# An adaLN transformer block on one core: all row tiles of the attention product in pairs, each pair by half-size products

## The chip, the cores and the metric

The kernel runs on one core of a Trainium2 chip. Its time is the device time of one execution in microseconds (us). Before the change it is 756.9 us (median of three runs, 756.22 to 757.13). The engines are TensorE (PE, with its weight loads shown apart as PEld), VectorE (DVE), ScalarE (ACT), GpSimd (POOL) and SyncE (SP, which here only issues transfers).

## The reference

For each of 8 batches, with x of 1024 rows by 256 columns, all in float32:

```python
mod = (_silu(c) @ wmod).reshape(8, 6, 1, 256)
sa, ca, ga, sb, cb, gb = (mod[:, n] for n in range(6))
ga, gb = (sign(g) * maximum(abs(g), 0.25) for g in (ga, gb))
h = layernorm(x) * (1 + ca) + sa
x = x + ga * (softmax((h * w_lhs) @ (h * w_rhs).T) @ h)
h = layernorm(x) * (1 + cb) + sb
x = x + gb * (relu(h @ W1 + b1) @ W2 + b2)
```

W1 is 256 by 1024, W2 is 1024 by 256. So one batch has a score matrix of 1024 by 1024, its softmax, the product of that with a 1024 by 256 matrix, and the two layers of the FFN.

## The kernel before, in words

**Stages.** A batch is cut into eight row tiles of 128 rows, i = 0 to 7 (`for b`, `for i` at the end of the kernel). In stage (b, i) the kernel computes the scores of the tile two ahead (`direct`, line 412), mirrors them into the part of the symmetric score matrix that was not computed (`mirror`, lines 435 and the transfer behind it), takes the row maximum (`row_max`, 463), turns it (`max_turn`, 468), subtracts (`subtract`, 475) and exponentiates (`exponent`, 484) the tile one ahead, and multiplies a tile's weights with the values (`xg`). The values carry a 257th column of ones, which gives the softmax's denominator. Beside this, in the same eight stages, runs the FFN of the batch before, one half of 512 rows (g = 0 or 1) in four stages: i = 0, 1 (and 4, 5) hold its first layer, two groups c each, and i = 2, 3 (and 6, 7) its second layer. Its result is turned back to rows and added to x some stages later (`y_gate`, `y_turn`, `y_add`, `y_out`). The next batch's normalisation and its turned copies (`prepare_norm` 281, `prepare_turn_apart` 342, `prepare_blocks` 322, `x_plus` and `xg_times` 642) are spread over the stages too.

**Products of weights and values.** A row tile can go alone: `product` (501) is 8 matmuls of 128 x 257, and `product_out` (513, 515) scales and adds on VectorE. Or two row tiles i and i+1 go together as a 2 x 2 block product by seven half-size products (a Strassen-Winograd scheme). `pair_begin` (549) computes two of the seven and ScalarE copies one (555); `pair_begin_sum` (561) adds them; `left_sums` forms four sums of the two weight tiles in place on GpSimd (565 and 575 to 577, 128 x 512 each); `pair_end` (593) computes the other five products with the sums of the values in `tsum` (`right_sums`, 534); `pair_out` (608 to 621) combines on VectorE; `pair_stats` takes the layer norm's statistics of both tiles. In the batches after the first, tiles 0 and 5 go alone, and (1, 2), (3, 4), (6, 7) are pairs. Batch 0 uses single products only.

**The FFN's first layer** goes by the same scheme, four groups c per half. `pair_products` computes six of seven products into `pa`, `pb`, `pc`; ScalarE copies `pa` into `kept` (747); `pair_sums` adds on VectorE (762, 765, 768, 771); `pair_last` writes the seventh product over the first half of `pa`, VectorE adds it (779), and GpSimd adds the fifth product, `kept[:, hi]`, to two halves of the result f with one instruction of 128 x 512 (780). `pair_relu` (789, 790) follows on ScalarE, and `pair_turn` (799 to 802) forms the second layer's sums on GpSimd. The second layer is `y_first` and `y_second` (806).

**What sets the order.** Each engine runs its instructions in the order of the program; `pin` adds that order as a dependency, so nothing is reordered. A buffer of the pool `ps_a` (four PSUM banks, shared by `pa`, `pb`, `pc`, `po`, `pp`, `pq`, `pr`, `ya` and the like) is given to the next tile when the last reader of the one four allocations earlier is done. `s1`, `W` and `f` have a single buffer each, `kept` and `u` two. Transfers of `move` are issued by SP in order: four writes to DRAM and one read back; with `hurry=False` the read is put off until after the next such transfer. GpSimd's adds of rows (`later`) wait in a queue from which `spare()` takes one at a time.

Of the kernel before, what the change touches and what calls it, by code (L numbers as in the profile page):

```python
# [11 lines left out]
F32 = mybir.dt.float32  # L12
AF = mybir.ActivationFunctionType
ALU = mybir.AluOpType
# [3 lines left out]
P = 128  # L18
# [6 lines left out]
def adaln_block_kernel(  # L25
# [435 lines left out]
    def row_max(b, i):  # L461
        m = work.tile([P, 1], F32, tag="m", name=f"m_{b}_{i}")
        nc.vector.tensor_reduce(m, score_row(b, i), AX.XY, ALU.max)  # L463
        max_t[b, i] = m
# [95 lines left out]
        rows = slice(P, P + XS)  # L560
        nc.vector.tensor_tensor(W[:, 0, rows], pp[:, XS : 2 * XS], W[:, 1, rows], ALU.add)

    def left_sum(b, i):
        s1 = two_t["s1"] = work.tile([P, TH, P], F32, tag="s1", name=f"s1_{b}_{i}", bufs=1)
        nc.gpsimd.tensor_tensor(s1, *halves(pT_t[b, i + 1]), ALU.add)

    def left_sums(b, i):


        if "s1" not in two_t:  # L570
            left_sum(b, i)
        (a11, a12), (a21, a22) = halves(pT_t[b, i]), halves(pT_t[b, i + 1])
        s1 = two_t["s1"]
# [154 lines left out]
    def pair_products(b, g, c, between=None):  # L728

        if c == 0:  # L730
            ffn["f"] = two.tile([P, NI, HALF], F32, tag="f", name=f"f_{b}_{g}", bufs=1)
            if b < B - 1:
                ffn["ft"] = two.tile([P, 3, NH, H2], F32, tag="ft", name=f"ft_{b}_{g}", bufs=1)
        hT, hs = ffn["hT", g]
        n = ts(c, P)
        s1, a22 = (w1[:, k, ds((c + NH) * P, P)] for k in range(2))

        pool, tag = (ps_s, "s") if b == B - 1 else (ps_a, "a")
        pa = ps_a.tile([P, HALF], F32, tag="a", name=f"pa_{b}_{g}_{c}")
# [7 lines left out]
        nc.scalar.copy(kept, pa)  # L747
        mm(pb[:, lo], w1s[:, 0, n], hs[:, 1])
        mm(pb[:, hi], w1s[:, 1, n], hs[:, 2])
        mm(pc[:, lo], w1[:, 1, n], hT[:, 1, lo])  # L750
        mm(pc[:, hi], a22, hT[:, 0, hi])
        if between:
            between()
        pairs[c] = pa, pb, pc, kept

    def pair_sums(b, g, c):
        pa, pb, pc, kept = pairs[c]
        f = ffn["f"]
        u = work.tile([P, H2], F32, tag="u", name=f"u_{b}_{g}_{c}", bufs=2)
        pairs[c] = pa, kept, u  # L760
        far = f[:, c + NH, hi]
        nc.vector.scalar_tensor_tensor(
            u, pb[:, lo], b1_col(c), kept[:, lo], ALU.add, ALU.add
        )
        nc.vector.scalar_tensor_tensor(  # L765
            far, pb[:, hi], b1_step[:, c : c + 1], u, ALU.add, ALU.add
        )
        nc.vector.scalar_tensor_tensor(
            f[:, c, lo], pc[:, lo], b1_col(c), kept[:, lo], ALU.add, ALU.add
        )  # L770
        nc.vector.tensor_tensor(f[:, c + NH, lo], pc[:, hi], far, ALU.add)

    def pair_last(b, g, c):


        pa, kept, u = pairs.pop(c)
        f = ffn["f"]
        mm(pa[:, lo], w1s[:, 2, ts(c, P)], ffn["hT", g][0][:, 1, hi])
        nc.vector.tensor_tensor(f[:, c, hi], pa[:, lo], u, ALU.add)  # L779
        nc.gpsimd.tensor_tensor(  # L780
            f[:, c::NH, hi],
            f[:, c::NH, hi],
            kept[:, None, hi].to_broadcast([P, 2, H2]),
            ALU.add,
        )

    def pair_relu(c):
# [362 lines left out]
    for b in range(B):  # L1150
        for i in range(NT):
# [63 lines left out]
            if first:  # L1215

                ub, ug = (b - 1, 0) if i >= TH else (b - 2, 1)
                back = i % TH == 0 and ub >= 0
                pair_products(fb, fg, c, turn_max)
                if i == 0:  # L1220
                    ffn_rstd(b - 1, 1)
                if i == 4:
                    y_gate(fb)
                    if b + 1 < B:
                        prepare_rstd(b + 1, 1)
                if i == TH + 1:
# [1 line left out]
                pair_sums(fb, fg, c)  # L1228
                if (b, i) == (1, 0):
                    subtract(*late)  # L1230
                if i == 4:
                    y_turn(fb, 0)
                if ahead:
                    mirror(*ahead)
                pair_last(fb, fg, c)
                if i == 0 and back:
                    for q in range(2):
                        y_add(ub, ug, q)
                if i == TH + 1:
                    pair_turn(c - 1)  # L1240
                if late and i != 4 and (b, i) != (1, 0):
                    subtract(*late)
                pair_products(fb, fg, c + 1, (lambda: max_turn(*extra)) if extra else None)
# [9 lines left out]
                        prepare_turn_apart(b + 1, 1, 0)  # L1253
                if i == 1:
                    exponent(*late)
                    left_sum(b, i)
                elif i == 4 and b + 1 < B:
                    prepare_norm(b + 1, 1)
                    x_plus(b + 1, 1)
# [15 lines left out]
                    weights(*late)  # L1275
                if ahead and ahead != extra:
                    row_max(*ahead)
                pair_turn(c)
                if i == 0:
                    pair_relu(c + 1)  # L1280
                    pair_turn(c + 1)
                if i == 4:
                    for q in range(2):
                        y_add(ub, ug, q)
                if c > 0:
                    pair_relu(c + 1)
                    pair_turn(c + 1)
            else:
                half = i % TH - 2
                if i == NT - 2:  # L1290
                    for q in (1, 3):
                        if (b, q) in two_t:
                            pair_stats(b, q)
                if i == 2:
                    left_sums(b, 1)
                elif i == 3:
                    pair_begin(b, i, turn_max)
                elif i == 6:
                    pair_begin(b, i, lambda: (max_turn(*late), weights(*late)))
                elif not ahead:  # L1300

                    pair_end(b, i - 1)
                    pair_out(b, i - 1)
                    pair_stats(b, i - 1)
                if half:
                    y_second(fb, fg, turn_max if i == NT - 1 else None)
                else:
                    y_first(fb, fg, turn_max if i == 2 else None)
                if ahead:
# [4 lines left out]
                    ffn_rstd(b, 0)  # L1314
                elif i == NT - 1 and b == B - 1:
                    ffn_rstd(b, 1)
                if i in (3, 6):
                    pair_begin_sum(b, i)
                if i == 2:
                    weights(*late)  # L1320
                elif i == 6:
                    left_sums(b, i)
                spare()
                early(b, i)
# [6 lines left out]
                if ahead:  # L1331
                    row_max(*ahead)
                if half:
                    y_second_sums(fb)
                    if i == NT - 1:
                        y_gate(fb)
                    elif b + 1 < B:
                        prepare_stats(b + 1, 1)
                else:
                    y_first_sums()  # L1340
                spare()
            if extra:
                subtract(*extra)
            if i == NT - 1 and 0 < b < B - 1:
                y_turn(fb, fg, True)
            turns(b, i)
            norms(b, i)
            if extra:
# [103 lines left out]
```

## Time and profile before

| | |
|---|---|
| median of three runs | 756.9 us (756.22 to 757.13) |
| the profiled execution | 756.93 us, span 755.1 us |
| TensorE busy | 749.1 us |
| VectorE busy | 574.9 us |
| GpSimd busy | 570.9 us |
| ScalarE busy | 374.9 us |
| one batch in the middle (253.26 to 343.70) | 90.44 us |

The page lists for each engine its busy time; the chain that ended last follows the work back from the end of the program, at each step to what released it; the groups of instructions give for each line the engine, the tiles (output <- inputs), the count, the busy time, the mean duration of one in ns and the idle time before it; the timeline lists single instructions with start and duration in us. A busy time counts an instruction's whole duration, and successive ones overlap a little, so that where the cost of one instruction more is wanted, the time from start to start is the better measure.

### The profile page before, as it was taken

The page shows a single profiled execution, that of the slowest core. Times are in us where ns is not written, and L with a number is a line of the kernel's source. Part 1 is how long each engine was busy: PE and PEld are TensorE (multiplying, and loading weights), DVE is VectorE, ACT ScalarE, POOL GpSimd, SP SyncE. Part 2 cuts the span into 40 slices and gives each one's busy share as a digit, 9 for nine tenths or more (in the row PEclk, how much of TensorE's full clock was granted, in tenths as well). Part 3 has the DMA queues.
Part 4 walks back from the last instruction along what each step waited for, and adds up shares of the span by engine and source line. Part 5 has one row for each costly group of instructions (what it writes and reads, how often), then busy time and mean ns, then how long its engine had stood idle before and what let it go on. Part 6 is the DMA issues. An engine that isn't in the chain of part 4 may idle for free.

```text
span 755.1 us, 11883 instructions
## 1 busy us (share of the span) xinstructions
PE 749.1 (99%) x3876; PEld 623.4 (83%) x3876; DVE 574.9 (76%) x1259; ACT 374.9 (50%) x688; POOL 570.9 (76%) x658
## 2 busy tenths in 40 slices
PE   8999999999999999999999999999999999999998
PEld 4686889788897888888888878988889788888887
DVE  7787879778796879968878688876889777685632
ACT  4554646635375454745546444563546535252521
POOL 3762796878968798788877699777996888669741
PEclk9999999999999999999999999999999999999999
DMA  9033442455443453445534555245553354133220
GB/s 308 16 112 98 131 133 74 135 178 152 127 120 123 153 153 110 147 118 158 164 99 119 153 154 161 74 127 172 155 152 85 119 166 133 50 91 126 84 85 28
DMA packets 106213, 95.21 MB, mean 126 GB/s; under 512 B 29700, under 2 KB 98848, under 8 KB 106152
## 3 DMA queue, kind: packets, MB, share of 16 engines
q1 hardware_dynamic: 98408, 85.81, 38.6%
q10 hardware_dynamic: 7744, 8.65, 3.7%
q8 instruction: 30, 0.49, 0.3%
q14 instruction: 31, 0.25, 0.1%
HBM read 50.62 MB, written 43.81 MB: 125 GB/s over the span
## 4 chain that ended last, share of the span: by engine, by line
PE 96%; DMA 1%; DVE 1%; ACT 1%; issue 0%
PE psc L412 16%; PE pa L726 11%; PE po L501 10%; PE pr L593 7%; PE pb L726 7%; PE pc L726 7%; PE yc L806 6%; PE ya L806 6%; PE yb L806 6%; PE pq L593 5%; PE pp L549 5%; PE py L916 4%; PE yd L806 3%; DMA wm<-in_L_wmod_dram 1%; PE pm L468 1%; PE pmr L194 0%
## 5 line engine op out<-in xcount | busy, mean ns | idle before, releaser
L412 PE MATMUL psc<-rT,lT 128*128 128x512 f32 (+3 forms) x384 | 134.8, 487 | 0.0
L780 POOL TENSOR_TENSOR f<-f,kept 128x512 f32<-128x512 f32 x64 | 81.5, 1274 | 42.8 <-DVE f L779 20.1
L419 ACT COPY sc<-psc 128x512 f32<-128x512 f32 (+3 forms) x96 | 44.7, 476 | 119.9 <-PE psc L412 113.0
L484 ACT ACTIVATE pT<-pT 128x1024 f32<-128x1024 f32 x64 | 67.6, 1056 | 70.6 <-DVE pT L475 70.5
L475 DVE TENSOR_TENSOR pT<-sc,pm 128x1024 f32<-128x1024 f32 x64 | 77.3, 1208 | 29.3 <-PE pm L468 13.7
L412 PEld LDWEIGHTS psc<-rT,lT 128*128 128x128 f32 x384 | 66.4, 191 | 37.2 <-issue 25.6
L501 PE MATMUL po<-xg,pT 128*128 128x257 f32 x352 | 80.6, 380 | 0.0
L463 DVE TENSOR_REDUCE m<-sc 128x1 f32<-128x1024 f32 x64 | 77.4, 1209 | 2.2 <-ACT sc L419 1.8
L501 PEld LDWEIGHTS po<-xg,pT 128*128 128x128 f32 x352 | 66.2, 190 | 10.0 <-issue 0.7
L747 ACT COPY kept<-pa 128x512 f32<-128x512 f32 x64 | 37.4, 584 | 69.3 <-PE pa L726 69.1
L726 PE MATMUL pb<-hs,w1s 128*128 128x256 f32 x256 | 65.9, 380 | 0.1
L726 PE MATMUL pc<-hT,w 128*128 128x256 f32 x256 | 65.7, 379 | 0.0
L880 POOL TENSOR_TENSOR x<-x,Y 128x512 f32<-128x512 f32 x28 | 35.1, 1276 | 29.3 <-DMA Y<-D_y 29.3
L789 ACT ACTIVATE f<-f 128x512 f32<-128x512 f32 x64 | 39.8, 622 | 34.7 <-POOL f L780 34.7
L642 POOL TENSOR_TENSOR x<-x,rows 128x256 f32<-128x256 f32 x64 | 44.8, 732 | 13.8 <-ACT rows L1022 10.6
L726 PEld LDWEIGHTS pb<-hs,w1s 128*128 128x128 f32 x256 | 48.5, 190 | 7.3 <-DVE f L765 0.8
L726 PEld LDWEIGHTS pc<-hT,w 128*128 128x128 f32 x256 | 48.6, 190 | 6.7
L806 PE MATMUL yc<-f,w2s 128*128 128x256 f32 x224 | 51.3, 379 | 0.0
L435 DVE STREAM_TRANSPOSE Tm<-sc 128x896 f32<-128x896 f32 (+6 forms) x49 | 34.3, 701 | 20.3 <-ACT sc L419 19.6
L806 PEld LDWEIGHTS yc<-f,w2s 128*128 128x128 f32 x224 | 41.5, 190 | 8.1 <-issue 2.9
L549 PEld LDWEIGHTS pp<-xg,pT 128*128 128x128 f32 x336 | 41.9, 192 | 5.1 <-DVE st_b L241 1.4
L799 POOL TENSOR_TENSOR ft<-f 128x256 f32<-128x256 f32 x56 | 40.8, 729 | 6.8 <-ACT f L790 6.8
(166 smaller groups left out, 1821.1 us busy)
## 6 DMA issues: line engine op xcount, KB each, us to landing
D_f<-T_f SPq DMA_DIRECT2D x60, 128.0 KB, 2.5
X_f<-D_f SPq DMA_DIRECT2D x15, 512.0 KB, 3.7
D_a<-T_a SPq DMA_DIRECT2D x56, 128.0 KB, 2.8
D_y<-T_y SPq DMA_DIRECT2D x56, 128.0 KB, 2.9
Y<-D_y SPq DMA_DIRECT2D x14, 512.0 KB, 3.4
out_dram<-x SPq DMA_DIRECT2D x14, 512.0 KB, 4.4
X_a<-D_a SPq DMA_DIRECT2D x13, 512.0 KB, 3.4
x<-in_L_attn_x_dram ACTq DMA_DIRECT2D x12, 512.0 KB, 3.4
```

The lines of the kernel that those rows point to most:

```text
L412: nc.tensor.matmul(psc[:, : hi - lo], lhsT=lT_t[b, i // TH][:, k, ts(i % TH, P)], rhs=rT_t[b, n][:, k, lo - n * HALF : HALF], start=(k == ...
L419: nc.scalar.copy(score_row(b, i)[:, lo // V : hi // V, :], psc[:, : hi - lo].rearrange("p (n v) -> p n v", v=V),)
L463: nc.vector.tensor_reduce(m, score_row(b, i), AX.XY, ALU.max)
L475: nc.vector.tensor_tensor(pT.rearrange("p j (a v) -> p j a v", v=V), score_columns(b, i), pm[:, :P].rearrange("p (j a v) -> p j a v", j=1, ...
L484: nc.scalar.activation(pT_t[b, i], pT_t[b, i], AF.Exp)
L501: nc.tensor.matmul(po[:, : D + 1], lhsT=pT[:, t, :], rhs=xg_t[b][:, t, 0 : D + 1], start=(t == 0), stop=(t == NT - 1),)
L549: nc.tensor.matmul(out, lhsT=lhs[:, t, :], rhs=xg_t[b][:, h * TH + t, P : P + XS], start=(t == 0), stop=(t == TH - 1),)
L593: nc.tensor.matmul(out, lhsT=lhs[:, t, :], rhs=rhs[:, t, :], start=(t == 0), stop=(t == TH - 1),)
L642: queue.append(lambda: nc.gpsimd.tensor_tensor(out, in0, row, op))
L726: nc.tensor.matmul(out, lhsT=lhsT, rhs=rhs, start=True, stop=True)
L780: nc.gpsimd.tensor_tensor(f[:, c::NH, hi], f[:, c::NH, hi], kept[:, None, hi].to_broadcast([P, 2, H2]), ALU.add,)
L806: nc.tensor.matmul(out, lhsT=lhs(c), rhs=rhs(c), start=(c == 0), stop=(c == NH - 1))
```

## The change

All eight row tiles of the batches after the first go in pairs: (0, 1), (2, 3), (4, 5), (6, 7). `left_sum` and `left_sums` become one function, called in i = 1, 2, 5, 6 for the pairs beginning at 0, 2, 4, 6. The first two products of a pair are computed in i = 0, 2, 4, 6 and the other five in i = 1, 3, 5, 7. To make room, the gate and the turn of the FFN's second half move from the end of i = 7 into i = 0 of the next batch, its addition to x (`y_add`) from i = 0 to i = 1 (and that of the first half from i = 4 to i = 5), the output one stage later, `right_sums` a little earlier in i = 7, and the statistics of each pair to stages where they are placed by hand. In the FFN, VectorE adds `kept[:, hi]` to `u` with one more instruction per group (new line 767), so that the seventh product's sum holds it; GpSimd's instruction then covers one half of f (128 x 256) and not two. Batch 0 keeps its single products.

```diff
-    def left_sum(b, i):
+    def left_sums(b, i):
         s1 = two_t["s1"] = work.tile([P, TH, P], F32, tag="s1", name=f"s1_{b}_{i}", bufs=1)
         nc.gpsimd.tensor_tensor(s1, *halves(pT_t[b, i + 1]), ALU.add)
-
-    def left_sums(b, i):
-        if "s1" not in two_t:
-            left_sum(b, i)
         (a11, a12), (a21, a22) = halves(pT_t[b, i]), halves(pT_t[b, i + 1])
...
         nc.vector.tensor_tensor(f[:, c + NH, lo], pc[:, hi], far, ALU.add)
+        nc.vector.tensor_tensor(u, kept[:, hi], u, ALU.add)
...
         nc.gpsimd.tensor_tensor(
-            f[:, c::NH, hi],
-            f[:, c::NH, hi],
-            kept[:, None, hi].to_broadcast([P, 2, H2]),
-            ALU.add,
+            f[:, c + NH, hi], f[:, c + NH, hi], kept[:, hi], ALU.add
         )
...
+                returned = i % TH == 1 and ub >= 0
                 pair_products(fb, fg, c, turn_max)
                 if i == 0:
                     ffn_rstd(b - 1, 1)
+                if back:
+                    y_gate(ub)
                 if i == 4:
-                    y_gate(fb)
...
                 pair_sums(fb, fg, c)
...
-                if i == 4:
-                    y_turn(fb, 0)
+                if back:
+                    y_turn(ub, ug)
                 if ahead:
                     mirror(*ahead)
+                if i % TH == 1:
+                    left_sums(b, i - 1)
                 pair_last(fb, fg, c)
-                if i == 0 and back:
-                    for q in range(2):
-                        y_add(ub, ug, q)
-                if i == TH + 1:
+                if i % TH == 1:
                     pair_turn(c - 1)
+                if (b, i) == (B - 1, 5):
+                    pair_stats(b, 2)
...
-                    left_sum(b, i)
...
+                if returned:
+                    for q in range(2):
+                        y_add(ub, ug, q)
                 pair_turn(c)
                 if i == 0:
                     pair_relu(c + 1)
-                    pair_turn(c + 1)
-                if i == 4:
-                    for q in range(2):
-                        y_add(ub, ug, q)
...
-                if i == NT - 2:
-                    for q in (1, 3):
-                        if (b, q) in two_t:
-                            pair_stats(b, q)
+                if i == NT - 2 and b < B - 1:
+                    pair_stats(b, 2)
                 if i == 2:
-                    left_sums(b, 1)
+                    pair_begin(b, i)
                 elif i == 3:
-                    pair_begin(b, i, turn_max)
+                    turn_max()
                 elif i == 6:
                     pair_begin(b, i, lambda: (max_turn(*late), weights(*late)))
-                elif not ahead:
-
+                else:
+                    turn_max()
                     pair_end(b, i - 1)
-                    pair_out(b, i - 1)
-                    pair_stats(b, i - 1)
+                    if not ahead:
+
+                        pair_out(b, i - 1)
+                        pair_stats(b, i - 1)
...
-                if i in (3, 6):
+                if not half:
                     pair_begin_sum(b, i)
-                if i == 2:
-                    weights(*late)
-                elif i == 6:
+                    if i == 2:
+                        weights(*late)
                     left_sums(b, i)
...
                 if half:
+                    if i == NT - 1 and ahead:
+                        pair_out(b, i - 1)
                     y_second_sums(fb)
-                    if i == NT - 1:
+                    if i == NT - 1 and b == B - 1:
                         y_gate(fb)
-                    elif b + 1 < B:
-                        prepare_stats(b + 1, 1)
+                    elif i == 3:
+                        pair_stats(b, 0)
+                        if b + 1 < B:
+                            prepare_stats(b + 1, 1)
                 else:
                     y_first_sums()
+                    if i == NT - 2:
+                        pair_stats(b, 4)
...
             if i == NT - 1 and 0 < b < B - 1:
-                y_turn(fb, fg, True)
+                while queue:
+                    spare()
+                right_sums(b + 1, range(4))
...
-            if i in (0, 5):
-                product(b, i)
-                product_out(b, i)
-            elif i == 1:
+            if i in (0, 4):
                 pair_begin(b, i)
                 pair_begin_sum(b, i)
-            elif i == 3:
-                left_sums(b, i)
-            elif i in (2, 4) or i == NT - 1 and ahead:
+            elif i in (1, 3, 5):
                 pair_end(b, i - 1)
                 pair_out(b, i - 1)
-                if i == NT - 1:
-                    assert not queue
-                    right_sums(b + 1, range(4))
-                if i == NT - 1 or b == B - 1:
-                    pair_stats(b, i - 1)
+            elif i == NT - 1 and ahead:
+                pair_stats(b, i - 1)
             late = ahead if ahead != extra else None
-            if first and back:
+            if first and returned:
                 y_out(ub, ug)
```

More of the change, by code (lines that the diff above doesn't have):

```diff
@@ L561, in pair_begin_sum @@
         nc.vector.tensor_tensor(W[:, 0, rows], pp[:, XS : 2 * XS], W[:, 1, rows], ALU.add)
-    def left_sum(b, i):
+    def left_sums(b, i):
         s1 = two_t["s1"] = work.tile([P, TH, P], F32, tag="s1", name=f"s1_{b}_{i}", bufs=1)
         nc.gpsimd.tensor_tensor(s1, *halves(pT_t[b, i + 1]), ALU.add)
-    def left_sums(b, i):
-        if "s1" not in two_t:
-            left_sum(b, i)
         (a11, a12), (a21, a22) = halves(pT_t[b, i]), halves(pT_t[b, i + 1])
-        s1 = two_t["s1"]
         add = nc.gpsimd.tensor_tensor
@@ L1289, in adaln_block_kernel @@
                 half = i % TH - 2
-                if i == NT - 2:
-                    for q in (1, 3):
-                        if (b, q) in two_t:
-                            pair_stats(b, q)
+                if i == NT - 2 and b < B - 1:
+                    pair_stats(b, 2)
                 if i == 2:
-                    left_sums(b, 1)
+                    pair_begin(b, i)
                 elif i == 3:
-                    pair_begin(b, i, turn_max)
+                    turn_max()
                 elif i == 6:
                     pair_begin(b, i, lambda: (max_turn(*late), weights(*late)))
-                elif not ahead:
+                else:
+                    turn_max()
                     pair_end(b, i - 1)
-                    pair_out(b, i - 1)
-                    pair_stats(b, i - 1)
+                    if not ahead:
+                        pair_out(b, i - 1)
+                        pair_stats(b, i - 1)
                 if half:
-                    y_second(fb, fg, turn_max if i == NT - 1 else None)
+                    y_second(fb, fg)
                 else:
```

## The prediction

> **What bounds the kernel now.** I read the page first, then the time by stages, then the rows around the edits.
>
> ```profile
> span 755.1 us, 11883 instructions
> PE   749.1 (99%) x3876; PEld 623.4 (83%) x3876; DVE 574.9 (76%) x1259; ACT 374.9 (50%) x688; POOL 570.9 (76%) x658
> PE 96%; DMA 1%; DVE 1%; ACT 1%; issue 0%
> ```
>
> TensorE (PE) is busy 99% and is 96% of the chain that ended last. So work taken off TensorE is time won, as long as nobody makes it wait, and every wait made for it is time lost. The other engines look loose, but only as averages. By stages (one batch from 343.70; i=0, 1, 4, 5 are the stages with the FFN's first layer):
>
> ```profile
> 343.70:355.90 12.20, 12.20 (x55) 9.95 (x54) 10.70 (x25) 5.85 (x12) 12.04 (x12) 1.00 0.52 151
> 355.90:366.01 10.11, 10.11 (x55) 8.37 (x53) 8.32 (x19) 5.80 (x11) 8.28 (x11) 1.00 0.68 201
> 366.01:379.21 13.20, 13.20 (x80) 11.36 (x78) 9.45 (x21) 6.30 (x13) 12.73 (x17) 1.00 0.46 128
> 387.58:399.06 11.48, 11.48 (x74) 10.60 (x73) 10.79 (x27) 8.43 (x16) 7.60 (x8) 1.00 0.22 55
> 399.06:409.13 10.07, 10.07 (x51) 8.87 (x50) 9.11 (x21) 5.93 (x11) 6.87 (x8) 1.00 0.71 214
> ```
>
> Columns: length, then busy time of PE, PEld, DVE, ACT, POOL, then clock. In i=0 and i=2 GpSimd (POOL) is full to 0.2 and 0.5 us, and in i=4 VectorE (DVE) to 0.7: little room for work that moves there. The period is 90.43 us, TensorE packed throughout.
>
> **The gain.** A whole product is 16 `po` records, 3.46 us from the first to the next group (352.44 to 355.90). A pair is 16 `pp` records, 1.78 us (364.22 to 366.01), and 40 `pq`/`pr` records, 4.46 us (374.75 to 379.21): 6.24 against 6.92 for two products. Products 0 and 5 go in batches 1 to 7, one more pair comes: 7 x 0.69 = 4.8 us. Batch 0 is unchanged. Without a wait, 756.9 - 4.8 = 752.1. The profiled execution took 756.93 us (span 755.1, 1.8 around it), the median 756.9, so both serve as one base.
>
> **GpSimd and VectorE, in sum.** GpSimd's add to f falls from 128x512 (1.27) to 128x256 (0.73), 8 per batch: -4.3. The fourth set of left sums adds four ops of 1.27 (1.33 with the turn-round): +5.3. Net +1 on some 74 of 90. VectorE gets eight adds L767 (u = kept + u, 128x256): nearest rows L771 and L779, 128x256, next start after 0.31 to 0.33, so 2.6; a pair_out (2.6, 399.55 to 402.17) and a W sum (0.2) for two product_outs (0.7 each): about +4 on 73. Neither is a bound as a sum; place decides. L767 has both inputs in SBUF, L771 not. VectorE rows with such inputs stretch while GpSimd works: L655 (128x4) took 143/408/1084 ns (min/median/max), and at 352.19 lasted 0.38, until just after GpSimd began another op at 352.51. So an L767 costs 0.31 to 0.31+1.27 (one GpSimd 128x512 op); I take 0.33, plus a lock where GpSimd's left sums run beside it.
>
> The Trainium skill ("SBUF — State Buffer", Who interferes with whom) says that a VectorE op with two SBUF inputs and a GpSimd op that reads SBUF exclude each other for a whole instruction. By that, with GpSimd 82% busy, each L767 would wait about half an op, an estimate of 0.5 us; by the row above mostly less.
>
> **Stages 4 and 5, the largest loss.** In i=5 TensorE's last product of c=2 (`pa`, w1s) overwrites a buffer that ScalarE (ACT) must first copy (`kept`). ScalarE's order is written out, and that copy stands behind a long row:
>
> ```profile
> 393.98 2.08 ACT L281 ACTIVATE xg<-x,rs,ra 128x256 f32<-128x256 f32 x4 [0.76 <-DVE rs L277]
> 395.97 0.61 ACT L789 ACTIVATE f<-f 128x512 f32<-128x512 f32 x1
> 397.01 1.50 ACT L342 ACTIVATE rT<-X_a,sides 128x512 f32<-128x512 f32 x2
> 398.42 1.51 ACT L342 ACTIVATE lT<-X_a,sides 128x512 f32<-128x512 f32 x2
> 399.83 1.04 ACT L484 ACTIVATE pT<-pT 128x1024 f32<-128x1024 f32 x1
> 400.77 0.24 ACT L419 COPY sc<-psc 128x128 f32<-128x128 f32 x1
> 400.92 0.58 ACT L747 COPY kept<-pa 128x512 f32<-128x512 f32 x1
> ```
> ```profile
> 402.21 0.60 PE L726 MATMUL pa<-hT,w1s 128*128 128x256 f32 x2
> ```
>
> The copy ends at 401.50, the product starts at 402.21: 0.7 us of slack. The change puts pp(4) (1.78) where pair_end (4.46) stood at the end of i=4, so TensorE comes there 2.68 earlier, counted from i=4's start. ScalarE does not: its row starts at `xg`, released by VectorE's rs, which stands behind one more L767 (0.31), and a copy of W (0.15) joins the row. The wait is 2.68 - 0.7 + 0.31 + 0.15 = 2.4. Behind that product on TensorE stand c=3 and pair_end(4): all slip. Then pair_end(4)'s `pq` needs the PSUM buffer that VectorE's sums of c=3 free; L767(c2) beside left_sums adds a little: 0.25, at worst one 1.27 op. I take 2.7 for the two stages; ends 2.0 (no further delay of rs, TensorE 0.4 later anyway) and 3.9 (2.4, a 1.27 lock, 0.25).
>
> **Stages 0 to 2.** y_turn of the second half comes from the end of i=7 to i=0: two transposes (1.22) on VectorE ahead of Tm, their five DMAs (four writes now, the read after) ahead of Tm's writes on SP. In i=4 the same order stands already: Tm there ends at 393.5, its read is issued at 398.28 and lands some 2.3 later (stage's median). Moved to i=0, Tm ends at 352.3, so its read lands near 359.5 and is wanted by the subtraction in i=1 at 362.2: no cost; up to 1 if the larger Tm (80 KB for 16 per write) lands late. VectorE from 348.28 (u of c=0), in order: four sums 1.71, L767 0.31, T_y 1.22, Tm 0.76, sum 0.31, subtraction 1.13, rs_f 0.30; c=1: 1.63+0.33+0.33; row maximum 1.13, T_f 1.23, W 0.21; c=2: 1.65+0.33; Tm 0.62, sum 0.31, subtraction 1.13; two ops of c=3 0.91: 15.55, to 363.83 without one wait. TensorE now does pair_end(0) at the end of i=1, and wants the buffer those two ops free at 363.71. With the waits for c=2's `kept` copy (359.17) and a lock at L767(c2) it is 0.7 late; and pp(0), behind L779's read of `pa` (352.66 for 352.44), waits 0.28. Together 0.98, ends 0 to 2.7 (two L767 locked by 0.9 each).
>
> GpSimd then: from 356.0 the smaller add of c=1 (0.73), a turn (2.98), left_sums(0) (5.3), 0.73, 2.98, 0.73, y_add 2.5 (moved here from i=0), 2.98, and the first two ops of c=3's turn 1.53: 20.5, with 0.5 of locks to 377.05. TensorE's fourth `ya` product reads that at about 375.4 plus the 0.98: 0.7 late. So 1.7 up to the end of i=2, ends 0.7 and 2.9. In before left_sums came after the last turn, behind nobody.
>
> The rest: right_sums (5.3 of GpSimd) moves to i=7, ahead of hs; hs is needed by `pb` in the next i=0, 3.45 us in, and done about 0.1 before: cost 0, up to 0.5 if that cover goes (inside the ends above). pair_stats (1.05 each) go to i=3, 6 and 7, where VectorE has 1.9 or more idle per stage: 0. y_out one stage later, the SP queue behind it has X_f's writes a stage off: 0.
>
> **Sum.** Batches 2 to 6: +1.7 +2.7 -0.69 = +3.7, together 18.6. Batch 1 has no y_turn and y_add of an earlier batch: 0.2+2.7-0.69 = 2.2. Batch 7 prepares no next batch, so no xg/rT/lT row: 1.7+0.5-0.69 = 1.5. Total +22: 779.
>
> On the clock: it is 1.00 in each stage. At the kernel's start, after idling, 128x512 matmuls (`pw`) took 1141 ns against 592 for `prow`. The Trainium skill ("TensorE: Matmul & The Clock Gate", HAM oscillation) says that a wait longer than its window, some 3.4 us, sends TensorE back to half clock. My longest wait is 2.4; so nothing is taken in. By the rule, at waits over 3.4, each would cost a few us more, an estimate.
>
> **Rivals.**
> 1. *Nothing waits: faster, 752.1.* For it: ScalarE is only 50% busy, and the sums of VectorE and GpSimd fit. It needs the `kept` copy of i=5 done 2.4 us earlier relative to i=4; if VectorE's rs came that much earlier (it stands behind c=0's sums, which start on TensorE's own pace), the sign turns. Against: ScalarE waited just 0.76 in that row, all the rest is its own work.
> 2. *Only the wait for `kept` stays.* VectorE and GpSimd catch up in their idle us of stages 1 to 3. Then 6 x 2.45 - 4.8 = +10: 767.
> 3. *Locks and contention are worse.* Eight more VectorE ops with two SBUF inputs per batch beside GpSimd; three of them on the path, each held by up to one us: 779 + 6 x 3 = 797.
> 4. *The pairs save nothing on TensorE* (the sum 6.24 not reached): same row in before's profile already, unlikely.
>
> **How the numbers follow.** Low end of my case: 6 x 2.0 + 6 x 0.7 - 4.8 = +11, 768; high 6 x (3.9+2.9) - 4.8 = +36, 793. Chances: my case 0.57 (768 to 793), rival 2 0.22 (762 to 768), rival 3 0.11, rival 1 0.09 with a hundredth for a gain and losses that cancel. 762 to 794 leaves out rivals 1 and 3, 0.2. No change means within 0.2%, 1.5 us, which is what a measurement of this kernel can tell. Faster 0.09, same 0.01, slower 0.90.
>
> **What the profile after would show.** TensorE's busy time some 5 us less, idle before `pa` L721 released by ACT `kept` in i=5 of batches 1 to 6, 2.4 each; small waits before `pq` (DVE) in i=1 and `ya` (POOL) in i=2; L767's mean over 0.4 us, its maximum over 1. I am wrong if ScalarE's `kept` ends ahead of TensorE's need in i=5, or if a wait I did not follow (hs, X_f, Tm's read) is longer than these.

## The result, and the profile after

The changed kernel takes 792.5 us (median of four runs, 791.3 to 793.3) against 757.0 for the kernel before on the same chip: 1.047 times as long, 95% interval 1.0452 to 1.0488. That is 35.5 us more; the prediction's likeliest value was 22 more. The page of the changed kernel, the lines that answer to those shown of before:

```profile
span 790.7 us, 12472 instructions
PE 758.2 (96%) x4044; PEld 626.3 (79%) x4044; DVE 621.0 (79%) x1358; ACT 374.8 (47%) x695; POOL 576.9 (73%) x686
PE 70%; DVE 13%; ACT 8%; issue 5%; DMA 3%; POOL 1%; SPq 0%; DVEq 0%; POOLq 0%; ACTq 0%
```

TensorE has fallen from 96% to 70% of the chain that ended last; VectorE (13%) and ScalarE (8%) now stand in it. The groups of waits of the changed kernel say where (engine, line, what for; us in total, how often, the longest):

```profile
PE pq L588 <- DVE f L760: 9.3, 12, 2.3
PE pa L721 <- ACT kept L742: 9.1, 8, 1.4
PE pm L468 <- DVE m L463: 4.5, 6, 0.8
PE pr L588 <- DVE f L775: 1.9, 7, 0.3
```

None of these four groups is among the waits of TensorE's matmuls of before. The stages of one batch (i = 0, 1, 2, 3, 4, 5; length, then busy PE, PEld, DVE, ACT, POOL, then the clock):

```profile
358.91:370.11 11.20, 11.05 (x55) 8.52 (x54) 8.60 (x21) 6.35 (x12) 3.60 (x5) 1.00 0.31 84
370.11:384.65 14.54, 13.28 (x79) 11.04 (x78) 13.78 (x29) 7.87 (x16) 12.96 (x15) 1.00 0.56 174
384.65:395.18 10.53, 10.53 (x56) 8.70 (x54) 7.37 (x19) 4.21 (x9) 9.08 (x13) 1.00 0.50 147
395.18:406.23 11.05, 11.05 (x71) 9.85 (x70) 10.25 (x25) 3.20 (x6) 10.74 (x14) 1.00 0.52 150
406.23:415.03 8.80, 8.80 (x51) 7.92 (x50) 7.95 (x22) 5.36 (x12) 2.92 (x5) 1.00 0.26 63
415.03:429.20 14.17, 11.82 (x76) 10.36 (x75) 12.05 (x21) 9.05 (x16) 12.22 (x15) 1.00 0.46 129
```

Only i = 1 and i = 5 leave TensorE idle to speak of (1.3 and 2.4 us), the two stages that now hold both groups c and the five products of a pair. In i = 1 VectorE is busy 13.78 of 14.54 us. GpSimd, full in i = 0 and i = 2 before, is idle two thirds of i = 0.

In numbers per batch, from TensorE's starts: what it takes from the start of one group of matmuls to the start of the next, less what the same step takes where nothing is waited for. In the batch shown that is 0.28 before `pp` and 0.42 before `pr`, 1.06 to 1.24 before `pq` in i = 1; 0.91 before `pm`, 1.66 before `pa` and 0.32 before `pq` in i = 5: 4.7 to 4.8. Some 0.5 lies in pieces under 0.15, most of them 0.1 at the first matmul behind a wait. Less the 0.69 that the pair saves, this is what the batch got longer by. Taken at the `pm` of i = 0, batch by batch, the changed kernel's excess over before is 5.0 (b = 1), 4.8, 5.8, 4.6, 5.6, 4.6 (b = 2 to 6), and 5.3 for b = 7 and the end: 35.7.

**i = 5.** TensorE's timeline there, in the changed kernel (start, duration, in brackets the idle time and what ended it):

```profile
417.21 1.03 PE L721 MATMUL pc<-hT,w 128*128 128x256 f32 x4
418.98 0.32 PE L468 MATMUL pm<-ident,m 128*128 128x128 f32 x1 [0.75 <-DVE m L463]
420.75 0.70 PE L721 MATMUL pa<-hT,w1s 128*128 128x256 f32 x2 [1.45 <-ACT kept L742]
```

and ScalarE's row that it waits for (four shorter instructions, at 415.01, 415.53, 419.81 and 419.96, are left out):

```profile
413.03 2.08 ACT L281 ACTIVATE xg<-x,rs,ra 128x256 f32<-128x256 f32 x4 [1.15 <-DVE rs L277]
416.05 1.50 ACT L342 ACTIVATE rT<-X_a,sides 128x512 f32<-128x512 f32 x2
417.46 1.50 ACT L342 ACTIVATE lT<-X_a,sides 128x512 f32<-128x512 f32 x2
418.87 1.04 ACT L484 ACTIVATE pT<-pT 128x1024 f32<-128x1024 f32 x1
420.12 0.58 ACT L742 COPY kept<-pa 128x512 f32<-128x512 f32 x1
```

The row from `xg` to the copy is nearly that of before (7.09 us from first to last start, 6.94 before). TensorE reaches it earlier and waits. Ahead of it, for 0.91, it waits for VectorE's row maximum, which ends at 418.93:

```profile
417.73 1.20 DVE L463 TENSOR_REDUCE m<-sc 128x1 f32<-128x1024 f32 x1
```

In the kernel before, the end of the row maximum and the `pm` that needs it were 2.5 us apart (399.63 and 402.10):

```profile
398.43 1.20 DVE L463 TENSOR_REDUCE m<-sc 128x1 f32<-128x1024 f32 x1
402.10 0.27 PE L468 MATMUL pm<-ident,m 128*128 128x128 f32 x1
```

**i = 1.** TensorE's two waits, then VectorE (three instructions ahead of the last one are left out) and, below it, GpSimd in the same microseconds:

```profile
378.85 1.13 PE L588 MATMUL pr<-tsum,s 128*128 128x128 f32 x8 [0.26 <-DVE f L775]
380.98 1.16 PE L588 MATMUL pq<-tsum,pT 128*128 128x128 f32 x8 [1.00 <-DVE f L760]
```
```profile
376.01 0.41 DVE L766 TENSOR_TENSOR f<-pc,f 128x256 f32<-128x256 f32 x1
376.34 1.43 DVE L767 TENSOR_TENSOR u<-kept,u 128x256 f32<-128x256 f32 x1
377.70 0.70 DVE L435 STREAM_TRANSPOSE Tm<-sc 128x512 f32<-128x512 f32 x1
380.44 0.48 DVE L760 SCALAR_TENSOR_TENSOR f<-pb,b_step,u 128x256 f32<-128x256 f32 x1
```
```profile
374.87 1.27 POOL L567 TENSOR_TENSOR s<-pT 128x512 f32<-128x512 f32 x1
376.22 1.27 POOL L570 TENSOR_TENSOR pT<-pT,pT 128x512 f32<-128x512 f32 x1
377.57 1.33 POOL L571 TENSOR_TENSOR pT<-s,pT 128x512 f32<-128x512 f32 x1
```

The new add takes 0.41 where GpSimd leaves it alone (all 64: 411/416/1441 ns, minimum, median, maximum). Here GpSimd's left sum (line 570) began 0.12 ahead of it, and it lasts until shortly after that one's end: 1.43. (This is what "lock" stands for below: the add is held while a GpSimd op runs.) The `f` of line 760 (c = 3), which frees `pq`'s buffer, ends at 380.9; TensorE takes `pq` up at 380.98.

### The profile page after: what moved, and what is told of

Its sections match the earlier page's. It is cut to its first block, busy times and chain, and to the rows that moved or that the text cites. A ratio compares the mean times of both kernels' runs of the same rounds, so it can differ in the third digit from the quotient of the medians.

```text
span 790.7 us, 12472 instructions
## 1 busy us (share of the span) xinstructions
PE 758.2 (96%) x4044; PEld 626.3 (79%) x4044; DVE 621.0 (79%) x1358; ACT 374.8 (47%) x695; POOL 576.9 (73%) x686
## 4 chain that ended last, share of the span: by engine, by line
PE 70%; DVE 13%; ACT 8%; issue 5%; DMA 3%; POOL 1%; SPq 0%; DVEq 0%; POOLq 0%; ACTq 0%
PE psc L412 14%; PE pr L588 8%; PE pq L588 7%; PE ya L799 6%; PE yc L799 6%; PE yb L799 6%; PE pa L721 4%; PE po L501 4%; PE pp L549 3%; PE pb L721 3%; PE yd L799 3%; DVE pT L475 2%; DVE f L760 2%; DVE u L757 2%; DVE u L767 2%
## 5 line engine op out<-in xcount | busy, mean ns | idle before, releaser
L776 POOL TENSOR_TENSOR f<-f,kept 128x256 f32<-128x256 f32 x64 | 48.5, 757 | 107.4 <-DVE f L766 107.4
L588 PE MATMUL pq<-tsum,pT 128*128 128x128 f32 (+1 forms) x448 | 60.4, 278 | 9.3 <-DVE f L760 9.3
L588 PEld LDWEIGHTS pq<-tsum,pT 128*128 128x128 f32 x448 | 54.5, 192 | 11.6 <-DVE f L760 11.6
L549 PEld LDWEIGHTS pp<-xg,pT 128*128 128x128 f32 x448 | 54.3, 192 | 10.2 <-issue 6.0
L549 PE MATMUL pp<-xg,pT 128*128 128x129 f32 x448 | 56.0, 276 | 0.9 <-DVE rs_f L650 0.2
L757 DVE SCALAR_TENSOR_TENSOR u<-pb,cols,kept 128x256 f32<-128x256 f32 x64 | 30.5, 477 | 27.1 <-PE pb L721 21.0
L721 PE MATMUL pa<-hT,w1s 128*128 128x256 f32 x128 | 39.5, 394 | 9.1 <-ACT kept L742 9.1
L567 POOL TENSOR_TENSOR s<-pT 128x512 f32<-128x512 f32 x28 | 35.7, 1274 | 16.7 <-ACT pT L484 16.7
```

What stands on the lines that cost most here:

```text
L549: nc.tensor.matmul(out, lhsT=lhs[:, t, :], rhs=xg_t[b][:, h * TH + t, P : P + XS], start=(t == 0), stop=(t == TH - 1),)
L588: nc.tensor.matmul(out, lhsT=lhs[:, t, :], rhs=rhs[:, t, :], start=(t == 0), stop=(t == TH - 1),)
L721: nc.tensor.matmul(out, lhsT=lhsT, rhs=rhs, start=True, stop=True)
L757: nc.vector.scalar_tensor_tensor(u, pb[:, lo], b1_col(c), kept[:, lo], ALU.add, ALU.add)
L776: nc.gpsimd.tensor_tensor(f[:, c + NH, hi], f[:, c + NH, hi], kept[:, hi], ALU.add)
```

## The experiments

Two theories at the start. The first: the loss is the order of the work, TensorE meeting ScalarE's row in i = 5 and VectorE's row in i = 1 too early, as predicted. The rival: the new VectorE add, held by GpSimd wherever it falls, is the larger cause. Later a third came up, GpSimd being late when the add is given back to it. Differences are to the kernel before, measured beside each run; for the changed kernel that is +35.5.

**One part alone.** The kernel before, with the add split between VectorE and GpSimd, and nothing else:

```diff
+        nc.vector.tensor_tensor(u, kept[:, hi], u, ALU.add)
...
         nc.gpsimd.tensor_tensor(
-            f[:, c::NH, hi],
-            f[:, c::NH, hi],
-            kept[:, None, hi].to_broadcast([P, 2, H2]),
-            ALU.add,
+            f[:, c + NH, hi], f[:, c + NH, hi], kept[:, hi], ALU.add
         )
```

> The kernel before with one part of the change alone: VectorE adds the fifth product to u, GpSimd to one half of f; tiles and pairs as before. If the time is lost by the pairs' order (ScalarE's row before the kept copy in i=5, VectorE's row before pq in i=1), this part alone costs little, since the kept copy has 0.7 us of slack in i=5 and VectorE has idle time around i=1: 756 to 760. If the locks between the new VectorE add and GpSimd are the cause, they are here too, beside the left sums of i=1: some 2 us per batch, 767 or more, with waits of TensorE in the same places.

Measured: 761.9 us, +4.2 (ratio 1.0054, 1.0037 to 1.0071), between the two expectations. Four of seven batches are 0.4 to 0.5 longer, two 0.8 and 0.9, the last one with the end 1.7. So most of the 35.5 is not this part, though it is no free part either. The same with the add reading the product from PSUM (`pa[:, hi]`), after the seventh product, in place of the SBUF copy:

```diff
-        nc.vector.tensor_tensor(u, kept[:, hi], u, ALU.add)
...
         mm(pa[:, lo], w1s[:, 2, ts(c, P)], ffn["hT", g][0][:, 1, hi])
+        nc.vector.tensor_tensor(u, pa[:, hi], u, ALU.add)
         nc.vector.tensor_tensor(f[:, c, hi], pa[:, lo], u, ALU.add)
```

> The kernel before with the fifth product's add on VectorE, read from PSUM and not from the kept copy; tiles and pairs as before. With the copy from SBUF this part alone cost 4.2 us. If that was the lock between the add and GpSimd: 757 or a little under, since GpSimd is relieved of 4.3 us per batch. If it was the VectorE time of eight more ops per batch (ahead of rs, pair_out and the row maximum): 760 to 762 again.

Measured: 760.5, +2.7 (1.0023 to 1.0053). The second expectation is the nearer. 1.5 of the 4.2 is gone, though the two intervals overlap: by the profiles two of the seven batches are 0.6 and 0.9 shorter than with the SBUF operand, and the 0.4 to 0.5 of the steady batches stays. TensorE's weight loads in both runs wait for VectorE's `pr` (line 611, six times, 2.2 and 2.4 us), which they did not before: VectorE's own time, in a stage that was full to 0.7 us.

**The other part alone.** The changed kernel with GpSimd adding to both halves of `f` again (the first diff, reversed):

> The changed kernel with GpSimd adding the fifth product to both halves of f again, and no new VectorE add: pairs alone. In i=0 and i=1 three adds of 0.33 and a lock of 1.1 leave VectorE's row ahead of pq: the waits before pr and pq (0.42 and 1.06 per batch) should go, 0.3 of the wait in i=5 as well: about -1.5 x 7, 782. If the locks are the larger cause: below 777. If GpSimd, with 4.3 us more per batch, becomes late for ya in i=2, as its row of 20.5 us said before: no gain, 790 or more, with TensorE waiting for POOL there.

Measured: 795.2, +37.6, so 2 us slower than with the split. The third expectation is the one that holds. The waits before `pr` are gone and those before `pq` fall to 0.35 in the batch shown above, but GpSimd is late instead, and ScalarE behind it: from the end of i = 0 on, where ScalarE's relu of c = 0 waits 2.71 for GpSimd's longer add (1.27), ScalarE's row is 1.3 later, and in i = 1 TensorE waits 1.07 for the `kept` copy of c = 2 in that row. TensorE's waits there:

```profile
PE pa L721 <- ACT kept L742: 16.5, 13, 1.7
PE ya L801 <- POOL ft L795: 3.8, 6, 0.9
PE pb L721 <- POOL hs L711: 3.5, 7, 0.7
PE pq L588 <- DVE f L760: 2.7, 6, 1.2
```

With four pairs the split is worth having; with three it is not. The pairs' order costs the time either way.

**ScalarE's row.** First by leaving work out: `lT` of the next batch's first half is not made, `rT` is used for it.

```diff
                 if sides_too:
-                    prepare_turn_apart(b + 1, 0, 0)
+                    lT_t[b + 1, 0] = rT_t[b + 1, 0]
```

> The changed kernel without the turned left copy of the next batch's first half (two activations, 1.41 us of ScalarE in i=4; the right copy is used in its place, so scores of batches 2 to 7 are not the reference's). If ScalarE's row sets the wait for the kept copy in i=5 (0.91 before pm and 1.66 before pa, 2.57 in all), it shrinks by 1.41 to the 0.9 to 1.2 that VectorE's row maximum also asks for: -1.4 x 6, 784. If the copy waits for something else, or the time comes back at pq right behind: 791 or more.

Measured: 786.8, +29.2. Then with nothing left out, `rT` moved ahead of the copy of c = 1, into ScalarE's idle time:

```diff
                     if b + 1 < B:
                         prepare_rstd(b + 1, 1)
+                        prepare_turn_apart(b + 1, 0, 1)
...
-                if sides_too:
-                    prepare_turn_apart(b + 1, 0, 1)
```

> The changed kernel with the next batch's turned right copy (rT, 1.41 us of ScalarE) ahead of the kept copy of c=1 in i=4, where ScalarE idles, and not behind the relu of c=0. Nothing is left out. If ScalarE's row alone sets the kept copy of i=5, this gains as much as leaving out lT did (-0.95 per batch and the lowered clock behind it): 787. If the copy of c=1, now 0.7 later, holds VectorE's sums, the shift is only passed on: 791 or more.

Measured: 785.1, +27.8. Both do the same to the wait: in the batch shown it is 0.92 before `pm` and 0.66 before `pa`, 1.58 for 2.57. ScalarE's row is thus shown to set the wait for `kept`, and VectorE's row maximum the first 0.9 of it. A part came back at `pq` right behind (0.32 became 0.53 to 0.55).

**The clock.** The gain of these two, 6 to 8 us, is more than six times 1.0 less 0.2. Part of the rest is TensorE's clock. The next lines are windows of 6 us from the seventh product of c = 2 in i = 5, two batches of the changed kernel, and the corresponding one of the run with `rT` early (after the busy times of PE, PEld, DVE, ACT and POOL comes the clock):

```profile
229.38:235.38 6.00, 5.84 (x35) 5.24 (x36) 5.83 (x12) 2.64 (x4) 5.76 (x6) 1.00 0.62 192
324.19:330.19 6.00, 6.00 (x23) 5.08 (x24) 5.39 (x12) 2.65 (x4) 5.76 (x6) 0.72 0.66 216
```
```profile
321.80:327.80 6.00, 5.63 (x33) 5.03 (x34) 5.82 (x12) 2.64 (x4) 5.76 (x6) 1.00 0.66 192
```

In the second line TensorE got through 23 matmuls in the time that another batch needs for 35, at a granted clock of 0.72. The wait ahead of it is the same 2.57 in both batches. Of the six batches with this wait, two were slowed in the changed kernel, and these two are the ones that are about 1 us longer than the others (5.8 and 5.6 over before, the others of b = 2 to 6 4.6 to 4.8). In the profiled executions of the two runs with a wait of 1.58 none was (three other executions of the run with `rT` early have a mean clock of 0.997 or 0.998, so a slowed stretch may lie somewhere in them).

What decides between the two shows when the trace is cut finer. These are three pieces of 3.41 us around the slowed batch:

```profile
320.95:324.36 3.41, 1.21 (x6) 0.59 (x5) 1.90 (x4) 3.41 (x8) 2.60 (x4) 1.00 0.40 62
324.36:327.77 3.41, 3.41 (x9) 2.70 (x10) 3.27 (x7) 1.42 (x3) 3.17 (x4) 0.50 0.79 264
327.77:331.18 3.41, 3.41 (x25) 3.20 (x24) 2.84 (x8) 1.06 (x1) 3.25 (x5) 1.00 0.46 154
```

The clock is halved for exactly one such piece. In the traces of all these runs, each slowed stretch that ends before the program does lasts 3.41 us, and those of one execution start whole multiples of 3.41 us apart (28 of them, 95.57 us, from batch to batch in the run with the add from PSUM below, whose batch takes 95.4). Cutting every trace at these multiples, the clock is halved behind each piece in which TensorE is listed idle for 1.87 us or more (21 pieces of six kernels) and behind none with 1.71 or less (some 3000; the first 30 us and the last 3 of each execution are left out). So the wait of 2.57 is punished where it falls into one piece, as above, and goes free where a cut divides it. The repairs of other waits that leave this one in place are therefore read with care, and at like clock:

**VectorE's row in i = 0 and 1.** y's gate and turn at the start of i = 0, where VectorE idles:

```diff
+                if back and i == 0:
+                    y_gate(ub)
                 pair_products(fb, fg, c, turn_max)
...
+                if back and i == 0:
+                    y_turn(ub, ug)
                 pair_sums(fb, fg, c)
...
-                if back:
+                if back and i == 4:
                     y_turn(ub, ug)
```

> The changed kernel with the gate and the turn of the FFN's second half at the start of i=0, ahead of the first sums, where VectorE idles 2.4 us (361.4 to 363.8), not behind them. If VectorE's row in i=0 and i=1 is what makes TensorE wait before pp, pr and pq there (0.28 + 0.42 + 1.06 = 1.76 per batch), its 1.22 us shorter row takes away about 1.2 of it in six batches: -7, 785. If the buffer's wait is set by the lock at L767 of c=2 alone, VectorE arrives early and waits there: no gain, 791 or more.

Measured: 792.5, +34.9: nothing in sum. In i = 1 of the batch shown, the wait before `pp` is gone and that before `pr` is 0.31, but that before `pq` is 1.06 as it was: VectorE comes early and stands at the add, as the second expectation has it. And five of six batches were slowed after the wait of i = 5, for two. A slowed batch is 5.1 us longer than before's in the mean here, and 5.7 in the changed kernel: some 0.5 gained per batch, given back to the clock. The add from PSUM (the second diff above) in the changed kernel:

> The changed kernel with VectorE's new add reading the fifth product from its place in PSUM (pa) and not from its SBUF copy (kept), right ahead of the seventh product's add: same sizes, one operand in another memory. If the lock between this add and GpSimd's left sums (1.43 us for 0.41, at c=2 of i=1) is what makes pq late there, it goes: about -1.1 for pq in i=1, 0.2 for pr, 0.3 in i=5, in seven batches: 783. If VectorE's row is too long without it too: -2 at most, 790 or more.

Measured: 790.8, +33.5. In i = 1 of the corresponding batch the wait before `pq` falls to 0.58 and that before `pr` goes, while that before `pp` grows to 0.40: 0.98 for 1.76 in i = 0 and 1, so the lock held about 0.8 of it. The sum hides this, since six of six batches were slowed (b = 2 to 6 are 4.9 to 5.0 longer than before's; the slowed ones of the changed kernel are 5.6 and 5.8). Last, the order of a pair's five products:

```diff
-            (pq[:, XS : XS + P], a22, tsum[:, 3, :, 0:P]),
             (pr[:, 2 * P : 3 * P], s3, tsum[:, 2, :, 0:P]),
+            (pq[:, XS : XS + P], a22, tsum[:, 3, :, 0:P]),
```

> The changed kernel with the products of pair_end in another order: the second and the third change places, so that pq is wanted 0.89 us later. If the wait for the PSUM buffer is the whole loss at pq, it falls from 1.06 to 0.2 in i=1 and from 0.32 to 0 in i=5: -1.2 x 7, 784. If VectorE is late for what follows as well (pair_out, the row maximum for the next pm), the same time turns up in i=2 and i=3: 790 or more.

Measured: 788.0, +30.7. TensorE waits for `pq` once in the whole run, not twelve times, and nothing turns up in i = 2 and 3. Of the 8 expected 4.5 are seen; five of six batches were slowed. The sixth shows what the repair is worth at full clock: it is 3.1 us longer than before's, where the changed kernel at full clock has 4.6 to 4.8, so 1.5 to 1.7 are gained, a little more than the 1.2 expected. The slowed ones are 4.6 and more. So in this kernel the halved clock costs 1.5 to 1.7 a batch; in the changed kernel about 1, where the 0.32 before `pq` behind it is gone in the slowed batches.

**All together**, and in i = 4 the subtraction and the row maximum ahead of the turn of xg:

> All the repairs together in the changed kernel: rT early, y's gate and turn at the start of i=0, the add from PSUM, pq one product later, and in i=4 the subtraction and the row maximum ahead of the turn of xg. If the waits named are all that the change costs (1.76 in i=0 and 1, 2.57 and 0.32 in i=5, the clock behind it), some 4.5 of 5.1 per batch go: 760 to 765, and 752 would be all of it. If they only hide others (the turned copy of xg lands later by 2.3 us, hs in i=0): 772 or more.

Measured: 768.6, +11.2 (1.0132 to 1.0166), clock 1.000. It falls between the two expectations: 24 of the 35.5 us are these waits and the clock behind them; no stretch of this execution is slowed. The wait for `kept` is still 1.30, and 0.42 to 0.71 for `hs`. Three more repairs for these:

```diff
+                if i == 5:
+                    exponent(b, 5)
...
-                    weights(*late)
+                    subtract(*late)
...
                         pair_out(b, i - 1)
+                        while queue:
+                            spare()
+                        right_sums(b + 1, range(4))
+                        turns(b, i)
                     y_second_sums(fb)
```

(the first two move the exponential of i = 4 behind the copy of c = 2; y's turn in i = 4 also goes behind VectorE's shift for xg.)

> All the repairs of the last run, and three more: in i=4 the exponential goes behind the kept copy of c=2 (0.95 us of ScalarE's row), VectorE's shift for xg goes ahead of y's turn (1.2), and in i=7 the turn of the FFN's input and its GpSimd sums hs go ahead of the second layer's last sums (1.4). If the waits left (1.30 for the kept copy, 0.42 to 0.71 for hs, per batch) were all, the pairs' gain of 0.69 per batch shows: 755 to 759, at the kernel before. If GpSimd's left sums or the transfers of y, both later now, become the next wait: 764 or more.

Measured: 766.5, +8.7. The waits named are gone; new ones of 0.64 (for VectorE's sum W, in i = 5) and 0.36 (for GpSimd, in i = 2) stand in their place, and 2.5 once in the last batch, with the clock halved behind it. Against these:

> The last version of the repaired pairs, with VectorE's sum of W ahead of the turn of xg in i=4 (TensorE waited 0.64 for it in i=5), and in the last batch the statistics of tiles 2 and 3 at the end of i=3 and the subtraction and exponential of i=6 behind the FFN's first products (TensorE waited 2.5 there once). If these waits end there: 766.5 - 6 x 0.6 - 3 = 760, still above before's 757.6, since GpSimd's 0.36 per half in i=2 and i=6 and hs at the end stay. If they are passed on: 764 or more.

Measured: 766.3, +8.5: passed on. With W earlier, the turn of xg comes between it and the sums of c = 2, and TensorE waits for these. VectorE and TensorE in this run:

```profile
402.68 0.28 DVE L561 TENSOR_TENSOR W<-pp,W 128x129 f32<-128x129 f32 x1
402.87 1.30 DVE L322 STREAM_TRANSPOSE T_a<-xg 128x512 f32<-128x512 f32 x2
404.09 0.45 DVE L757 SCALAR_TENSOR_TENSOR u<-pb,cols,kept 128x256 f32<-128x256 f32 x1
404.57 0.48 DVE L760 SCALAR_TENSOR_TENSOR f<-pb,b_step,u 128x256 f32<-128x256 f32 x1
```
```profile
405.11 1.13 PE L721 MATMUL pb<-hs,w1s 128*128 128x256 f32 x4 [0.52 <-DVE f L760]
```

Six of its seven batches are 0.5 to 0.9 longer than before's, and the last one with the end 4.9. The last run is the same kernel with the add from the SBUF copy again:

> The same kernel with the new VectorE add reading the SBUF copy (kept), as the change has it, and not PSUM. Nothing is lowered in clock here, so the difference is the price of the lock with GpSimd alone. If the lock is on TensorE's path in i=1 and i=5 (0.5 to 1.1 per batch): 4 to 8 us above the run beside it. If the other repairs have made enough room for it: within 1.5.

Measured: 769.5 (769.29 to 769.69) against 766.3 (765.73 to 766.57) beside it, both at full clock: 3.2 us, 0.5 per batch in the mean, between the two expectations. That is the price of the SBUF operand, together with the add's place, which is a little earlier in VectorE's row here (ahead of `Tm`, not behind the seventh product). That the operand is what lets GpSimd hold the add is to be read from its 64 durations (ns, least, median, longest), with `kept` in this run and with PSUM in the run beside it:

```profile
L767 DVE TENSOR_TENSOR u<-kept,u x64: 412/416/1437, 78.3 to 752.1; 128x256 f32<-128x256 f32 x64
L774 DVE TENSOR_TENSOR u<-pa,u x64: 382/412/425, 80.2 to 748.9; 128x256 f32<-128x256 f32 x64
```

No version with all tiles in pairs came under the kernel before.

## Why the prediction was right, and where it was short

The direction, the range and the two largest mechanisms held; the size was 13 us short. The upper end of its own case, 793, was built from longer waits in six like batches, some 6 us each with the pair's gain taken off. Those six came to 30.4, about 2 of it the clock, and the last batch to 5.3; for the clock and the last batch that end has nothing. That the time stayed inside, by 0.5 us, is in part luck. By its own steps:

- *The pair saves 0.69 per batch.* By starts yes: 1.78 for `pp` (413.25 to 415.03), 0.89 for each of the five groups. The marker named for it, TensorE's busy time 5 us lower, was wrong: it rose from 749.1 to 758.2. Each wait adds the modelled end of the matmul ahead of it (the wait before `pr` costs 0.42 by starts and is listed as 0.26 idle), and the slowed stretches count as busy.
- *Stages 4 and 5: 2.4 for `kept`, 0.25 for `pq`.* Measured 2.57 and 0.32. What was not named is that the first 0.9 of it is a wait for VectorE's row maximum; so shortening ScalarE's row alone gave 1.0 and not 1.4.
- *Stages 0 and 1: 0.98.* Measured 1.8 to 1.9. `pp`'s 0.28 was right to the digit. The term that was too small is the lock at the add of c = 2: it and the wait for the `kept` copy ahead of it were given 0.6 together, while the add alone took 1.0 longer (1.43 for 0.41), of which about 0.8 came through to TensorE. The bound named for one lock, 1.27, would have held it. Without the lock (the add from PSUM) these waits were 0.98, so VectorE's row was also later by itself than the forecast had it.
- *Stage 2: 0.7 for GpSimd's turns.* Not there in the changed kernel. It did appear, at 0.9 and 0.4, in the runs in which GpSimd had more to do or TensorE came earlier.
- *Batch 1: 2.2.* Measured 5.0. The step "has no y_turn and y_add of an earlier batch" failed: the waits before `pr` and `pq` are there in batch 1 as well (0.50 and 1.06, with 0.35 before `pp` and 0.38 before `pa`), and moving y's turn away left `pq`'s wait as it was. They do not hang on the turn, and on the lock in part: with the add from PSUM `pr`'s is gone and `pq`'s is 0.74.
- *Batch 7: 1.5.* Measured 5.3 with the end. The step that failed is "pair_stats ... to i=3, 6 and 7 ...: 0". In the last batch the change puts them into i = 5, among the sums that free `pq`'s buffer. With the lock beside them that wait is 2.49, once (1.76 with the add from PSUM; no run moves the statistics alone); 0.8 each for `ya` and `hs` comes on top, of which before had 0.5 and 0.2.
- *The clock: nothing taken in*, the longest wait, 2.4, being held too short for it. The Trainium skill ("TensorE: Matmul & The Clock Gate", HAM oscillation) describes TensorE falling back to half clock when waits cross its window, which Part 1 of the page gives as 3.4 us and free-running. The traces agree on the half clock, on the 3.41 us and on its running freely: the slowed stretches lie on multiples of it, whatever the length of a batch. They do not agree that a wait has to be as long: two waits of 0.91 and 1.66 with one small matmul between were enough in two batches of six, and in five and six of them in the kernels beside it; a single one of 2.51 was enough in the last batch of one more. What counted was 1.87 us of listed idle time or more within one 3.41. It cost about 1 us each time in the changed kernel.
- *The rivals.* Rival 3, the locks, was half right: one add per batch is held on the path, not three. Rival 2, only `kept`, falls with the waits of i = 1. Rival 1 needed a `kept` copy 2.4 us earlier; the runs with ScalarE's row shortened show that VectorE stands right behind it.

Taken together: batches 2 to 6 came to 25.4 for 18.6. Of these 6.8 about 2 are the clock and about 4 the waits in i = 0 and 1 (1.76 and more for 0.98), as much as the lock was seen to cost there; the 0.7 per batch for GpSimd that did not come is about made up by the pieces under 0.15. Batches 1 and 7 came to 10.3 for 3.7.

## What to carry to other kernels

When work is taken from the engine that bounds a kernel, it arrives earlier at every hand-over behind; ask at each how many microseconds of slack there were, not how busy the other engine is. ScalarE was busy half of the time and still made TensorE wait in each batch, since its order was fixed and its row had 0.7 us to spare. First and last batches are to be walked by their own code, not by subtracting what a steady batch has more.

## What the runs showed of the hardware

A VectorE op of 128x256 with two SBUF inputs takes 0.41 us alone and up to 1.44 beside a GpSimd op of 128x512, lasting until shortly after that one's end. With one input in PSUM it never took more than 0.425, and the whole kernel was 3.2 us faster at the same clock; this is the rule of the Trainium skill ("SBUF — State Buffer", Who interferes with whom), seen here with its price.

Unexpected was the clock. Two waits of 2.57 us together halve it for 3.41 us in some batches and not in others, depending on where they fall in a raster of 3.41 us that runs by itself: 1.87 us of idle time within one piece of it was enough, 1.71 was not. A batch of the run with the add from PSUM takes 95.4 us, nearly 28 pieces, and each of the six batches with this wait was hit. Small repairs elsewhere move the waits against the raster; they changed how many batches were hit, from two to six of six, and so hid what they gained. The mean clock of an execution tells little of this (0.987 to 0.996 in the four kernels with two to six such batches); the window behind each wait does.
